# Product 4 of the first layer by seven blocks of its own, and the sums of slots made by GpSimd

## The chip, the cores and the metric

The kernel runs on one core of one Trainium2 chip. Its time is the device time of one execution in microseconds; three runs are shown, and the median counts. Five engines work side by side [...]: TensorE (PE, its weight loads PEld), VectorE (DVE), ScalarE (ACT), GpSimd (POOL) and SyncE (SP), which here only issues transfers. Each engine takes its instructions in the order of the program.

## The reference

All data are float32. The input x has 4096 tokens of 512 numbers. Two quaternion products and a filter, which is one number per channel, come down to a 4 x 4 matrix per channel (`M` in the kernel) that mixes the four quarters of a token. The result goes into a mixture of 8 experts, each token to two of them:

```
xf = rotate(x)                                  # 4096 x 512
scores = softmax(xf @ gate_w.T); topv, topi = top_k(scores, 2)
gates = topv / sum(topv)
# every expert takes up to 1024 slots; tokens beyond that are dropped
h  = relu(de[e] @ fc1_w[e].T + fc1_b[e])        # 1024 x 2048, de[e]: slots of expert e
eo = h @ fc2_w[e] + fc2_b[e]                    # 1024 x 512
out = x + sum over the two experts of gate * eo
```

## The kernel before

A first part chooses the experts and makes the lists of slots. Then come 32 groups k = 4 e + g: expert e (0 to 7) and quarter g (0 to 3) of the 2048 hidden columns. Each group has a first layer (512 hidden columns for 1024 slots) and a second layer.

**Seven products for eight.** Both layers cut their matrices into 2 x 2 blocks and make seven block products instead of eight, after Winograd's form of Strassen's method. The factors are blocks or sums of blocks: sums of weights `s` (`left1`, line 132) and of slots `x` (`sums`, line 119, called by `Slots.factors`) for the first layer, and of second weights `t` (`right2`, line 177) and hidden values (`chain`, line 811) for the second. The sums of `left1`, `sums` and `right2` are made by GpSimd, those of `chain` by VectorE.

**Seven within one of seven.** In the first layer, products 1, 6, 3 and 2 are cut once more (`pair`, line 878): each is made of seven matmuls of 128 x 128 by 256 columns (`within`, line 835). Their sums of weights come from `left_sub` (line 146, GpSimd, four of 128 x 128 per product and group) and their sums of slots from `right_sub` (line 162, VectorE, four of 128 x 256 per product and expert). Products 0, 5 and 4 are plain: four matmuls of 512 columns each (`half`, line 856).

**Banks and additions.** Matmuls write into PSUM banks of 512 columns; the first layer has four (`bank1`). A term that several blocks of the result share is accumulated on in the same bank: TensorE writes term after term, and after each VectorE adds the bank to the blocks that want it (`add`, line 890; line 905 adds one bank to two pairs). TensorE may write the next term into a bank only when the addition before has read it. The blocks of the result lie in `beside` (three per group, two groups in turn: h11, h21, r12) and in one of five tiles `unused` (h22). `chain` then makes the three sums s1, s2, s4 that the second layer needs, in four additions of VectorE.

**The order of the work** is written by hand. `first_layers` is a generator with 14 units per group (0 to 3: products 0 and 5; 4 to 7: 1 and 6; 8, 9: 4; 10 to 13: 3 and 2), `second_layers` one with 7 steps for each half of the slots, so 14 per group as well. Group 0 is plain throughout (`layer1_plain`, line 940). The loop at line 1256 takes one unit and one step in turn, and the second layer is one group and about three units behind. After each unit and each step `turn` (line 789) issues so many closures from the list `background` as the table `PACE` (line 1244) says for this group and unit, and always one from the list `fetches`:

- `background` holds the additions of `chain` (put in front), the rotation of the next expert's slots (`Slots.steps`: transposes and multiply-adds of VectorE, 18 for each half), the weights of the slots (`weights`) and the stores (`store`: ScalarE weighs, GpSimd adds 128 x 512 and issues a scatter).
- `fetches` holds the transfers: gathers by GpSimd (choices, rows of the output, the next expert's slots), the load of the second bias, and the exchange between partitions (four transfers of SP each, line 707). `arrivals` (line 714) puts in gathers and exchanges of the next expert's slots in one go, with empty closures between.

Sums of weights and slots are issued in fixed units: `later` (line 1052) gives the units of `left_sub` and `right_sub`, `TURN_OF_SUM` those of `left1`; the four sums of `right2` are issued in steps 13 and 14, which fall in units 1 and 2 of the next group.

Of the kernel before, what the change touches and what calls it, by code (L numbers as in the profile page):

```python
# [39 lines left out]
P = 128  # L40
# [26 lines left out]
def kernel(  # L67
# [94 lines left out]
    def right_sub(pool, e, n, block):  # L162

        t = pool.tile([P, 4, HS], F32, tag=f"xsub{n}", name=f"xsub{n}_{e}")

        def b(c, h):
# [3 lines left out]
            lambda: V.tensor_tensor(t[:, 0], b(0, 1), b(0, 0), ALU.subtract),  # L170
            lambda: V.tensor_tensor(t[:, 1], b(1, 1), t[:, 0], ALU.subtract),
            lambda: V.tensor_tensor(t[:, 2], b(1, 1), b(0, 1), ALU.subtract),
            lambda: V.tensor_tensor(t[:, 3], b(1, 0), t[:, 1], ALU.subtract),
# [440 lines left out]
    beside = [hp.tile([P, 3, 2, HALF], F32, name=f"beside{i}") for i in range(2)]  # L614
    unused = [hp.tile([P, 2, HALF], F32, name=f"hidden{i}") for i in range(5)]
# [60 lines left out]
    class Slots:  # L676
# [37 lines left out]
        def arrivals(self, half):  # L714

            n = PER if half == 0 else 2
            t = self.a if half == 0 else self.b
            for at in range(0, PER, n):
                for st in range(n):
                    yield lambda st=st, at=at: self.gather_ahead(t[:, st], half, at + st)  # L720
                yield from [lambda: None] * 2
                for b in range(QT):
                    yield lambda b=b, at=at: self.exchange(t, half, at, b)
                yield from [lambda: None] * 2
# [71 lines left out]
    def product2(out, st0, factors, n, first, tiles=range(2)):  # L796
# [11 lines left out]
        if st0 + 2 == PER and 1 in tiles and n in (2, 3, 4, 5):  # L808
            unused.append(factors[0][n])

    def chain(k, h22):


        h11, h21, r12 = (beside[k % 2][:, i] for i in range(3))
# [3 lines left out]
        def last():  # L818
# [7 lines left out]
            *[lambda: None] * (2 if k == NK - 1 else 0),  # L826
            last,
        ]

# [16 lines left out]
    def layer1(k, factors, subs):  # L846
# [5 lines left out]
        h11, h21, r12 = (h[:, i] for i in range(3))  # L852
# [25 lines left out]
        def pair(n, o, at, base, base_read):  # L878
# [3 lines left out]
            two = h[:, at : at + 2]  # L882
            t, u = bank1(f"t{n}_{k}"), bank1(f"u{n}_{k}")
            halves = t.rearrange("p (n s) -> p n s", n=2)

            def both(bank, i, first=False):
                within(bank[:, A], subs, n, i, first)
                within(bank[:, B], subs, o, i)
# [38 lines left out]
        for m in range(2):  # L927
            half(b[m], m, 4, True)
            V.tensor_tensor(h22[:, m], b[m], h21[:, m], ALU.add)
            if m == 1:  # L930
                from4(1)
                relu(h22)
# [379 lines left out]
```

## Time and profile before

| | |
|---|---|
| median of 3 runs | 1564.13 us (1563.52 to 1565.92) |
| the profiled execution | 1567.49 us |
| its span, first to last instruction | 1565.7 us |
| mean granted TensorE clock | 0.989 |
| VectorE: L892, 128x512, bank and SBUF | 248 of 687 ns |
| VectorE: L905, 128x1024, bank to two pairs | 62 of 1225 ns |
| VectorE: sums of slots L170, L171, 128x256 | 16 + 16 from x: 887 and 1247 ns; least 415 |
| GpSimd: L155 to L158, 128x128 | 463 to 830 ns |
| GpSimd: L137 to L140, 128x512 | 1272 to 1282 ns |
| GpSimd: L125 to L128 on x, 128x1024 | 2354 to 2360 ns |
| GpSimd: gather of rows L601, scatter L657 | 64 of 996, 64 of 1095 ns |

The busy time in the profile counts instructions of an engine without the issue of registers and semaphores; starts of successive matmuls, not their printed lengths, give TensorE's pace, since matmuls overlap. A line such as L837 is that of a helper, so groups are told apart by the tiles named. "A <- B" in the lists of waits says that A stood until B was done; such releasers are inferred.

### The profile page before, as it was taken

Reading aid. Unit: us, or ns where it says so; the run is one execution under the profiler, and the core shown is the slowest. Engines: PE = TensorE matmul, PEld = TensorE weight load, DVE = VectorE, ACT = ScalarE, POOL = GpSimd, SP = SyncE. Lnnn points to the kernel's source line nnn. Section 1 sums busy time; section 2 is a strip of 40 time slices with the busy share of each in tenths; the row PEclk is TensorE's granted clock in tenths of the full one; section 3 lists DMA queues with packets and bytes.
Section 4 is the critical chain, followed back from the end, with each engine's and each line's share of the span. In section 5 each row is a group of like instructions: output and inputs, shape, how many; then the busy total and the mean of one; then the engine's idle time right before and its main releaser. Section 6 shows DMA issues by size and latency. Waiting matters only on the chain.

```text
span 1565.7 us, 17505 instructions
## 1 busy us (share of the span) xinstructions
PE 1531.0 (98%) x6399; PEld 1186.9 (76%) x6399; DVE 1152.8 (74%) x1608; ACT 316.6 (20%) x446; POOL 1045.9 (67%) x1129
## 2 busy tenths in 40 slices
PE   5899999999999999999999999999999999999997
PEld 2677777877877777877877777887777877777776
DVE  6667887588866888578885888758886688866656
ACT  3222211211131211221122221221212211121110
POOL 1763687755977478865779567785687747886453
PEclk7899999999999999999999999999999999999999
DMA  8463113421335203441135311442123511321021
GB/s 325 150 215 101 55 61 122 121 81 55 96 106 144 65 28 114 124 118 55 54 95 166 96 55 32 137 130 86 55 79 115 145 41 55 114 94 67 0 82 53
DMA packets 79374, 152.18 MB, mean 97 GB/s; under 512 B 12022, under 2 KB 40950, under 8 KB 74168
## 3 DMA queue, kind: packets, MB, share of 16 engines
q1 hardware_dynamic: 56848, 90.24, 18.6%
q0 software_dynamic: 18048, 52.31, 10.8%
q10 hardware_dynamic: 4392, 8.52, 1.4%
q8 instruction: 50, 0.82, 0.2%
q14 instruction: 36, 0.29, 0.1%
HBM read 119.77 MB, written 25.23 MB: 93 GB/s over the span
## 4 chain that ended last, share of the span: by engine, by line
PE 87%; DVE 6%; DMA 2%; issue 2%; POOL 1%; another core or an unknown queue 1%; SPq 1%; POOLq 0%; DVEq 0%
PE a L800 26%; PE b L800 19%; PE t L837 13%; PE a L858 11%; PE u L837 7%; PE b L858 7%; PE b L837 2%; PE a L837 1%; DMA xb<-in_xt_dram 1%; DVE hidden L824 1%; DVE xa L771 1%; PE p L959 1%; DVE hidden L820 1%; SPq L707 1%
## 5 line engine op out<-in xcount | busy, mean ns | idle before, releaser
L800 PE MATMUL a<-t,hidden 128*128 128x256 f32 x1024 | 242.0, 379 | 0.1
L892 DVE TENSOR_TENSOR beside<-t,beside 128x512 f32<-128x512 f32 x248 | 170.3, 687 | 92.3 <-PE t L837 88.1
L800 PEld LDWEIGHTS a<-t,hidden 128*128 128x128 f32 x1024 | 194.5, 190 | 53.0 <-issue 27.5
L833 ACT ACTIVATE beside<-beside 128x1024 f32<-128x1024 f32 x62 | 65.5, 1057 | 556.8 <-DVE beside L892 535.1
L837 PE MATMUL t<-xsub,sub 128*128 128x256 f32 x496 | 128.1, 381 | 0.9 <-DVE beside L892 0.2
L800 PEld LDWEIGHTS b<-w,hidden 128*128 128x128 f32 x504 | 95.8, 190 | 39.0 <-issue 29.2
L800 PE MATMUL b<-w,beside 128*128 128x256 f32 x512 | 121.0, 379 | 0.6 <-DVE acc L1224 0.6
L800 PE MATMUL a<-t,beside 128*128 128x256 f32 x512 | 120.9, 379 | 0.0
L800 PE MATMUL a<-w,beside 128*128 128x256 f32 x512 | 120.9, 379 | 0.0
L800 PE MATMUL b<-t,hidden 128*128 128x256 f32 x504 | 119.1, 379 | 0.0
L800 PE MATMUL b<-w,hidden 128*128 128x256 f32 x504 | 119.1, 379 | 0.0
L800 PEld LDWEIGHTS b<-w,beside 128*128 128x128 f32 x512 | 97.2, 190 | 27.3 <-issue 15.8
L800 PEld LDWEIGHTS a<-w,beside 128*128 128x128 f32 x512 | 97.3, 190 | 26.4 <-issue 14.8
L858 PE MATMUL b<-x,s 128*128 128x512 f32 x248 | 116.5, 592 | 0.0
L858 PE MATMUL a<-x,s 128*128 128x512 f32 x248 | 116.5, 592 | 0.0
L858 PE MATMUL a<-xa,w 128*128 128x512 f32 x248 | 116.4, 592 | 0.0
L137 POOL TENSOR_TENSOR s<-w 128x512 f32<-128x512 f32 x31 | 39.5, 1274 | 112.5 <-PE b L858 112.5
L139 POOL TENSOR_TENSOR s<-w 128x512 f32<-128x512 f32 x31 | 39.7, 1282 | 109.7 <-PE t L837 109.6
L140 POOL TENSOR_TENSOR s<-w,s 128x512 f32<-128x512 f32 x31 | 39.4, 1272 | 107.5 <-PE t L837 96.7
L800 PEld LDWEIGHTS a<-t,beside 128*128 128x128 f32 x512 | 97.3, 190 | 13.2
L837 PEld LDWEIGHTS t<-xsub,sub 128*128 128x128 f32 x496 | 93.6, 190 | 16.3 <-DVE beside L892 3.4
L800 PEld LDWEIGHTS b<-t,hidden 128*128 128x128 f32 x504 | 95.8, 190 | 13.0
(228 smaller groups left out, 3084.9 us busy)
## 6 DMA issues: line engine op xcount, KB each, us to landing
w<-in_w_dram SPq DMA_DIRECT2D x64, 1024.0 KB
xb<-in_xt_dram SPq DMA_DIRECT2D x8, 1024.0 KB
out_dram<-in_x_dram ACTq DMA_DIRECT2D x1, 8192.0 KB
rows<-xa SPq DMA_DIRECT2D x112, 64.0 KB
rows<-xb SPq DMA_DIRECT2D x224, 32.0 KB
b<-in_b_dram POOLq DMA_DIRECT2D x8, 256.0 KB
c<-choice,slot_cho POOLq DMA_INDIRECT x64
rows<-out_dram,slot_tok POOLq DMA_INDIRECT x64
```

The source lines that it names most:

```text
L137: lambda: G.tensor_tensor(s[0], w[:, 1, 0], w[:, 1, 1], ALU.add),
L139: lambda: G.tensor_tensor(s[2], w[:, 0, 0], w[:, 1, 0], ALU.subtract),
L140: lambda: G.tensor_tensor(s[3], w[:, 0, 1], s[1], ALU.subtract),
L707: nc.sync.dma_start(slots_of[half][q * CW : (q + 1) * CW, at : at + t.shape[1], b * P : (b + 1) * P], t[b * CW : (b + 1) * CW, :, q * P : ...
L771: V.scalar_tensor_tensor(to, t, M[:, i, j : j + 1], to, ALU.mult, ALU.add)
L800: nc.tensor.matmul(out[m] if isinstance(out, list) else out[:, m], lhsT=factors[0][n][:, c, (st0 + m) * P : (st0 + m + 1) * P], rhs=factor ...
L820: V.tensor_tensor(s4, h21, s2, ALU.subtract)
L824: lambda: V.tensor_tensor(s2, s1, h11, ALU.subtract),
L833: nc.scalar.activation(h, h, AF.Relu)
L837: nc.tensor.matmul(out, lhsT=subs[0][n][i], rhs=subs[1][n][i], start=first, stop=True, skip_group_check=True,)
L858: nc.tensor.matmul(out, lhsT=factors[0][n][:, c, m * P : (m + 1) * P], rhs=factors[1][n][:, c, :], start=first and c == 0, stop=c == 1, sk ...
L892: V.tensor_tensor(to, halves, to, ALU.add)
```

## The change

- `layer1` is written out anew. Product 4 is made of its own seven blocks (`singles`, `within`): in units 8 to 11, in banks `b` and `t4`, whose terms go into both blocks that want them (h22 and r12) by additions of VectorE that read the same 256 columns twice (`add_to_both`). Products 3 and 2 follow in units 10 to 13, partly in the same units. Steps of two terms into one bank stand in front of one addition where the blocks allow it (`singles` of two products into `b`).
- `beside` holds four blocks per group (h11, h22, h21, r12) and `unused` three tiles. ScalarE copies the second half of h21 into h22.
- In `chain` the last addition (s4) is no longer put in `background` with the three others; it waits in `waiting` until product 2 of the group before has been issued.
- `right_sub` is made by GpSimd, and there is one for product 4 too, as there is a `left_sub`. Their units change, as do those of `left1`.
- `arrivals` becomes `arrive`: gathers and exchanges of the next expert's slots are put in at units of their own, by the table `ARRIVE`; from the second expert on, four gathers of half 0 at (g 0, unit 3), two of half 1 at (0, 6), the first exchange at (0, 13). The rotation is put in at (1, 7) and (2, 6).
- `PACE` changes, and group 1 takes the row of g=1.

```diff
--- before.py
+++ after.py
@@ -161,16 +161,17 @@
     def right_sub(pool, e, n, block):
+        G = nc.gpsimd
         t = pool.tile([P, 4, HS], F32, tag=f"xsub{n}", name=f"xsub{n}_{e}")
         def b(c, h):
             return block[:, c, h * HS : (h + 1) * HS]
         steps = [
-            lambda: V.tensor_tensor(t[:, 0], b(0, 1), b(0, 0), ALU.subtract),
-            lambda: V.tensor_tensor(t[:, 1], b(1, 1), t[:, 0], ALU.subtract),
-            lambda: V.tensor_tensor(t[:, 2], b(1, 1), b(0, 1), ALU.subtract),
-            lambda: V.tensor_tensor(t[:, 3], b(1, 0), t[:, 1], ALU.subtract),
+            lambda: G.tensor_tensor(t[:, 0], b(0, 1), b(0, 0), ALU.subtract),
+            lambda: G.tensor_tensor(t[:, 1], b(1, 1), t[:, 0], ALU.subtract),
+            lambda: G.tensor_tensor(t[:, 2], b(1, 1), b(0, 1), ALU.subtract),
+            lambda: G.tensor_tensor(t[:, 3], b(1, 0), t[:, 1], ALU.subtract),
         ]
         return [b(0, 0), b(1, 0), b(1, 1), t[:, 3], t[:, 0], t[:, 1], t[:, 2]], steps
@@ -611,8 +612,8 @@
-    beside = [hp.tile([P, 3, 2, HALF], F32, name=f"beside{i}") for i in range(2)]
-    unused = [hp.tile([P, 2, HALF], F32, name=f"hidden{i}") for i in range(5)]
+    beside = [hp.tile([P, 4, 2, HALF], F32, name=f"beside{i}") for i in range(2)]
+    unused = [hp.tile([P, 2, HALF], F32, name=f"hidden{i}") for i in range(3)]
     stored, turned_of = {}, {}
@@ -711,17 +712,17 @@
                     t[b * CW : (b + 1) * CW, :, q * P : (q + 1) * P],
                 )
-        def arrivals(self, half):
+        def arrive(self, half, part):
+
             n = PER if half == 0 else 2
             t = self.a if half == 0 else self.b
-            for at in range(0, PER, n):
-                for st in range(n):
-                    yield lambda st=st, at=at: self.gather_ahead(t[:, st], half, at + st)
-                yield from [lambda: None] * 2
-                for b in range(QT):
-                    yield lambda b=b, at=at: self.exchange(t, half, at, b)
-                yield from [lambda: None] * 2
+            at = part // 2 * n
+            if part % 2 == 0:
+                return [
+                    lambda st=st: self.gather_ahead(t[:, st], half, at + st) for st in range(n)
+                ]
+            return [lambda b=b: self.exchange(t, half, at, b) for b in range(QT)]
         def turn_squares(self, half, j, t):
             V.transpose(
@@ -805,13 +806,17 @@
                     stop=c == 1,
                     skip_group_check=True,
                 )
-        if st0 + 2 == PER and 1 in tiles and n in (2, 3, 4, 5):
+        if st0 + 2 == PER and 1 in tiles and n in (2, 4, 5):
             unused.append(factors[0][n])
-
-    def chain(k, h22):
-
-
-        h11, h21, r12 = (beside[k % 2][:, i] for i in range(3))
+            if n == 2 and waiting:
+                background.insert(0, waiting.pop())
+
+    waiting = []
+
+    def chain(k):
+
+
+        h11, h22, h21, r12 = (beside[k % 2][:, i] for i in range(4))
         s1, s2 = unused.pop(0), unused.pop(0)
         hidden[k] = [h11, h21, None, h22, s1, s2, r12]
@@ -823,9 +828,8 @@
             lambda: V.scalar_tensor_tensor(s1, r12, 0.0, h22, ALU.max, ALU.add),
             lambda: V.tensor_tensor(s2, s1, h11, ALU.subtract),
             lambda: V.scalar_tensor_tensor(r12, r12, 0.0, h11, ALU.max, ALU.subtract),
-            *[lambda: None] * (2 if k == NK - 1 else 0),
-            last,
         ]
+        (waiting if k else background).append(last)
     hidden = {}
@@ -875,64 +879,95 @@
                 nc.scalar.activation(h21[:, m], a[m], AF.Identity, bias=hi[:, m : m + 1])
             yield
-        def pair(n, o, at, base, base_read):
...
+        def singles(bank, n, first=False):
+            within(bank[:, A], subs, n, 1, first)
+            within(bank[:, B], subs, n, 2)
+
+        def both(bank, n, o, i, first=False):
+            within(bank[:, A], subs, n, i, first)
+            within(bank[:, B], subs, o, i)
+
+        def add(two, m, half, bank):
+            to = two[:, :, m, half]
+            V.tensor_tensor(to, bank.rearrange("p (n s) -> p n s", n=2), to, ALU.add)
+
+        def add_twice(two, bank):
             to = two[:, :, :, B]
-            term = u.rearrange("p (n s) -> p n s", n=2).unsqueeze(2).to_broadcast([P, 2, 2, HS])
+            term = bank.rearrange("p (n s) -> p n s", n=2).unsqueeze(2).to_broadcast([P, 2, 2, HS])
             V.tensor_tensor(to, term, to, ALU.add)
-            yield
-            both(t, 6)
-            add(1, B)
-            within(u[:, A], subs, n, 1, True)
-            within(u[:, B], subs, n, 2)
-            V.tensor_tensor(two[:, 0, 0], u, two[:, 0, 0], ALU.add)
-            yield
-            both(t, 3)
-            add(1, A)
-            relu(two[:, 0])
-
-        def from5(m):
-            nc.scalar.activation(h21[:, m], a[m], AF.Identity, bias=hi[:, m : m + 1])
-
-        def from4(m):
-            V.tensor_tensor(r12[:, m], b[m], r12[:, m], ALU.add)
-
-        yield from pair(1, 6, 0, a[0], lambda: from5(0))
+
+        def add_to_both(two, m, half, term):
+
+            to = two[:, :, m, half]
+            V.tensor_tensor(to, term.unsqueeze(1).to_broadcast([P, 2, HS]), to, ALU.add)
+
+        def add_pair(one, bank):
+            V.tensor_tensor(one[:, 0], bank, one[:, 0], ALU.add)
+
+
+
+        two = h[:, 0:3:2]
+        t, u = bank1(f"t1_{k}"), bank1(f"u1_{k}")
+        singles(a[0], 6)
+        nc.scalar.activation(h21[:, 0], a[0], AF.Identity, bias=hi[:, 0:1])
+        both(t, 1, 6, 0, True)
+        add(two, 0, A, t)
         yield
-        h22 = unused.pop(0)
-        b = [bank1(f"b{m}_{k}") for m in range(2)]
-        for m in range(2):
-            half(b[m], m, 4, True)
-            V.tensor_tensor(h22[:, m], b[m], h21[:, m], ALU.add)
-            if m == 1:
-                from4(1)
-                relu(h22)
-            yield
-        yield from pair(3, 2, 1, b[0], lambda: from4(0))
-        chain(k, h22)
+        both(t, 1, 6, 5)
+        add(two, 0, B, t)
+        both(u, 1, 6, 4, True)
+        add_twice(two, u)
+        yield
+        both(t, 1, 6, 6)
+        add(two, 1, B, t)
+        singles(u, 1, True)
+        add_pair(h11, u)
+        yield
+        both(t, 1, 6, 3)
+        add(two, 1, A, t)
+        relu(h11)
+        yield
+        nc.scalar.activation(h22[:, 1], h21[:, 1], AF.Copy)
+        two = h[:, 1:4:2]
+        b, t4 = bank1(f"b_{k}"), bank1(f"t4_{k}")
+        singles(b, 4, True)
+        V.tensor_tensor(h22[:, 0], b, h21[:, 0], ALU.add)
+        within(t4[:, A], subs, 4, 0, True)
+        add_to_both(two, 0, A, t4[:, A])
+        yield
+        within(t4[:, A], subs, 4, 5)
+        within(t4[:, B], subs, 4, 4)
+        add_to_both(two, 0, B, t4[:, A])
+        to = two[:, :, :, B]
+        term = t4[:, B].unsqueeze(1).unsqueeze(1).to_broadcast([P, 2, 2, HS])
+        V.tensor_tensor(to, term, to, ALU.add)
+        yield
+        three = h[:, 2:4]
+        t, u = bank1(f"t3_{k}"), bank1(f"u3_{k}")
+        singles(b, 2)
+        within(t4[:, A], subs, 4, 6)
+        add_to_both(two, 1, B, t4[:, A])
+        both(t, 3, 2, 0, True)
+        add_pair(r12, b)
+        add(three, 0, A, t)
+        yield
+        within(t4[:, A], subs, 4, 3)
+        add_to_both(two, 1, A, t4[:, A])
+        relu(h22)
+        both(t, 3, 2, 5)
+        add(three, 0, B, t)
+        both(u, 3, 2, 4, True)
+        add_twice(three, u)
+        yield
+        both(t, 3, 2, 6)
+        add(three, 1, B, t)
+        singles(u, 3, True)
+        add_pair(h21, u)
+        yield
+        both(t, 3, 2, 3)
+        add(three, 1, A, t)
+        relu(h21)
+        chain(k)
         yield
     PAIRS = (slice(0, 2 * P), slice(2 * P, 4 * P))
...
@@ -1023,8 +1057,26 @@
         left_f, w1_t = None, None
         w1_of = {}
         lefts, right_subs = {}, {}
-        TURN_OF_SUM = {8: 2, 9: 0, 10: 1, 13: 3}
+        TURN_OF_SUM = {8: 2, 11: 0, 12: 1, 13: 3}
         nxt = None
+        ARRIVE = (
+            {
+                (0, 5): [(0, 0)],
+                (1, 0): [(0, 1)],
+                (1, 2): [(1, 0)],
+                (1, 5): [(1, 1)],
+                (1, 9): [(1, 2)],
+                (1, 12): [(1, 3)],
+            },
+            {
+                (0, 3): [(0, 0)],
+                (0, 6): [(1, 0)],
+                (0, 13): [(0, 1)],
+                (1, 6): [(1, 1)],
+                (1, 10): [(1, 2)],
+                (1, 13): [(1, 3)],
+            },
+        )
         for k in range(NK):
             e, g = divmod(k, NG)
             if k + 1 < NK:
@@ -1055,13 +1107,19 @@
             if k:
                 for n, block, turns in (
-                    (2, left_f[2], (2, 2, 3, 3)),
-                    (3, w1_of[k][:, 1, 1], (4, 4, 5, 5)),
+                    (4, left_f[4], (2, 2, 3, 3)),
+                    (2, left_f[2], (4, 4, 5, 5)),
+                    (3, w1_of[k][:, 1, 1], (6, 6, 7, 7)),
                 ):
                     lefts[n], more = left_sub(k, n, block)
                     later(more, turns)
                 if k == 1 or g == 0:
-                    for n, turns in ((6, (1, 2, 2, 3)), (2, (4, 4, 5, 5)), (3, (6, 7, 8, 9))):
+                    for n, turns in (
+                        (6, (2, 2, 3, 3)),
+                        (4, (3, 4, 4, 5)),
+                        (2, (2, 4, 7, 10)),
+                        (3, (3, 5, 8, 10)),
+                    ):
                         right_subs[n], more = right_sub(xtp, e, n, xf[n])
                         later(more, turns)
                 if k == 1:
@@ -1077,13 +1135,15 @@
                 if k:
                     if i == 8 and k + 1 < NK:
-                        lefts[6], more = left_sub(k + 1, 6, left_n[6])
-                        later(more, (9, 10, 11, 12))
-                        lefts[1], more = left_sub(k + 1, 1, w1_of[k + 1][:, 0, 1])
-                        later(more, (10, 11, 12, 13))
+                        for n, block, turns in (
+                            (1, w1_of[k + 1][:, 0, 1], (8, 8, 9, 9)),
+                            (6, left_n[6], (9, 10, 10, 11)),
+                        ):
+                            lefts[n], more = left_sub(k + 1, n, block)
+                            later(more, turns)
                         if g == NG - 1:
                             right_subs[1], more = right_sub(xtp, e + 1, 1, xf_n[1])
-                            later(more, (8, 9, 9, 12))
+                            later(more, (8, 10, 10, 12))
                     for f in ahead[i]:
                         f()
                 if k == 0 and i == 2:
@@ -1096,9 +1156,9 @@
                     nc.scalar.dma_start(*(a.rearrange("(b r) d -> r b d", r=PT) for a in (out, x)))
                 if e + 1 < E:
-                    if (g, i) in ((0, 12 if e else 5), (1, 8)):
-                        fetches.extend(nxt.arrivals(g))
-                    if (g, i) in ((1, 11), (2, 9)):
+                    for part in ARRIVE[e > 0].get((g, i), ()):
+                        fetches.extend(nxt.arrive(*part))
+                    if (g, i) in ((1, 7), (2, 6)):
                         background.extend(nxt.steps(g - 1))
                 if k and left_n and i in TURN_OF_SUM:
@@ -1242,10 +1302,9 @@
     PACE = (
-        [(1, 1)] * 2 + [(0, 1)] * 4 + [(0, 0)] + [(0, 1)] * 5 + [(1, 1), (0, 0)],
-        [(1, 1)] * 4 + [(1, 1), (0, 2), (0, 0), (0, 1), (1, 1)] + [(0, 1)] * 3 + [(1, 1), (0, 0)],
-        [(1, 1)] * 2 + [(2, 1)] * 2 + [(1, 2), (0, 2), (0, 0), (0, 1), (1, 1)]
-        + [(0, 1)] * 3 + [(1, 1), (0, 0)],
+        [(1, 1)] * 2 + [(1, 1)] * 4 + [(0, 0)] + [(0, 1)] * 5 + [(1, 1), (0, 0)],
+        [(1, 1)] * 4 + [(1, 2), (0, 2), (0, 0), (0, 1), (0, 1), (0, 0), (1, 1), (0, 0), (1, 1), (0, 0)],
+        [(1, 1)] * 2 + [(2, 1)] * 2 + [(1, 2), (1, 1), (0, 0), (0, 1), (0, 1), (0, 0), (1, 1), (0, 0), (1, 1), (0, 0)],
     )
     with tc.manual_schedule():
@@ -1261,7 +1320,7 @@
                     going = True
                 k, i = now
-                turn(1 if k in (0, NK - 1) else PACE[0 if k == 1 else min(k % NG, 2)][i][n])
+                turn(1 if k in (0, NK - 1) else PACE[min(k % NG, 2)][i][n])
         while background:
             turn()
```

More of the change, by code (lines that the diff above doesn't have):

```diff
@@ L851, in layer1 @@
         h = beside[k % 2]
-        h11, h21, r12 = (h[:, i] for i in range(3))
+        h11, h22, h21, r12 = (h[:, i] for i in range(4))
         A, B = slice(0, HS), slice(HS, HALF)
@@ L876, in layer1 @@
             yield
-        def pair(n, o, at, base, base_read):
[L882 to L888, printed above, removed]
-            def add(m, half):
-                to = two[:, :, m, half]
-                V.tensor_tensor(to, halves, to, ALU.add)
-            within(base[:, A], subs, o, 1)
-            within(base[:, B], subs, o, 2)
-            base_read()
-            both(t, 0, True)
-            add(0, A)
-            yield
-            both(t, 5)
-            add(0, B)
-            both(u, 4, True)
+        def singles(bank, n, first=False):
+            within(bank[:, A], subs, n, 1, first)
+            within(bank[:, B], subs, n, 2)
@@ L923, in layer1 @@
-        yield from pair(1, 6, 0, a[0], lambda: from5(0))
-        yield
-        h22 = unused.pop(0)
-        b = [bank1(f"b{m}_{k}") for m in range(2)]
-        for m in range(2):
-            half(b[m], m, 4, True)
-            V.tensor_tensor(h22[:, m], b[m], h21[:, m], ALU.add)
-            if m == 1:
-                from4(1)
-                relu(h22)
-            yield
-        yield from pair(3, 2, 1, b[0], lambda: from4(0))
-        chain(k, h22)
+        def add_to_both(two, m, half, term):
+            to = two[:, :, m, half]
+            V.tensor_tensor(to, term.unsqueeze(1).to_broadcast([P, 2, HS]), to, ALU.add)
@@ L943, in layer1_plain @@
         lo, hi = (b1_sb[:, e, g * 4 + 2 * a : g * 4 + 2 * a + 2] for a in range(2))
-        h11, h21, r12 = (beside[k % 2][:, i] for i in range(3))
-        h22 = unused.pop(0)
+        h11, h22, h21, r12 = (beside[k % 2][:, i] for i in range(4))
         for half in range(2):
@@ L977, in layer1_plain @@
                 if half == 1 and done:
-                    chain(k, h22)
+                    chain(k)
                 if len(parts) == 1 or i % 2:
```

## The prediction

> **What bounds the kernel now.** I read the head of the page first, then TensorE's waits, then the order of time on TensorE, then the busy time by group, and last GpSimd's order of time, since most of what the change moves goes there.
>
> ```profile
> span 1565.7 us, 17505 instructions
> PE 1531.0 (98%) x6399; PEld 1186.9 (76%) x6399; DVE 1152.8 (74%) x1608; ACT 316.6 (20%) x446; POOL 1045.9 (67%) x1129
> ```
>
> TensorE is busy for 98% of the span. The list of its own waits (total us, times, longest) holds start-up and almost nothing else:
>
> ```profile
> PE lt L359 <- DMA xb<-in_xt_dram: 12.7, 7, 6.8
> ...
> PE b L837 <- DVE hidden L929: 1.4, 1, 1.4
> ```
>
> So the time is TensorE's number of columns, and whatever makes it wait is added in full. Its order of time gives the price (start us, us, engine, line; the printed us overlap in the pipeline, so I take differences of starts; one float32 matmul is two records):
>
> ```profile
> 405.35 1.88 PE L858 MATMUL a<-xa,w 128*128 128x512 f32 x4
> ...
> 432.08 1.88 PE L858 MATMUL b<-x,s 128*128 128x512 f32 x4
> 433.79 1.89 PE L800 MATMUL a<-t,hidden 128*128 128x256 f32 x8
> 435.52 1.88 PE L858 MATMUL b<-x,s 128*128 128x512 f32 x4
> 437.24 1.89 PE L800 MATMUL b<-w,hidden 128*128 128x256 f32 x8
> 438.96 0.59 PE L837 MATMUL b<-xb,s 128*128 128x256 f32 x2
> 439.39 0.59 PE L837 MATMUL b<-xb,sub 128*128 128x256 f32 x2
> ...
> 451.91 1.88 PE L858 MATMUL a<-xa,w 128*128 128x512 f32 x4
> ```
>
> One group k (14 units of layer 1 laced with 14 steps of layer 2) takes 451.91 - 405.35 = 46.56 us. Two matmuls of 512 columns take 433.79 - 432.08 = 1.71 us, one of 256 takes 0.43 us, a step of layer 2 (four of 256) 1.73 us. Busy time by group (stretch: us, then PE, PEld, DVE, ACT, POOL):
>
> ```profile
> 405.40:451.90 46.50, 46.50 (x193) 36.43 (x192) 35.55 (x49) 9.69 (x14) 37.02 (x38) 1.00 0.33 107
> 451.90:498.50 46.60, 46.60 (x194) 36.51 (x193) 26.90 (x35) 12.20 (x18) 37.79 (x43) 1.00 0.49 142
> 498.50:545.00 46.50, 46.38 (x191) 35.78 (x190) 39.71 (x51) 9.00 (x14) 21.43 (x26) 1.00 0.25 73
> ```
>
> The first is group k=8, the first group of an expert (g=0). There GpSimd has 37 busy us of 46.5, and its DMA issues have gaps of about 0.3 us besides. This is the place that decides, so here it is in order of time:
>
> ```profile
> 405.10 2.36 POOL L128 TENSOR_TENSOR x<-xa,x 128x1024 f32<-128x1024 f32 x1
> 407.42 2.25 POOL L125 TENSOR_TENSOR t<-w 128x512 f32<-128x512 f32 x1
> ...
> 414.82 0.46 POOL L156 TENSOR_TENSOR sub<-sub,s 128x128 f32<-128x128 f32 x1
> 415.24 2.25 POOL L128 TENSOR_TENSOR t<-w,t 128x512 f32<-128x512 f32 x1
> ...
> 428.44 0.95 POOL L601 DMA_INDIRECT rows<-out_dram,slot_tok  x1 [0.30 <-issue]
> 429.70 0.95 POOL L601 DMA_INDIRECT rows<-out_dram,slot_tok  x1 [0.30 <-issue]
> 430.64 0.61 POOL L1121 DMA_DIRECT2D b<-in_b_dram  x1
> ...
> 440.75 1.27 POOL L673 TENSOR_TENSOR rows<-acc,rows 128x512 f32<-128x512 f32 x1 [1.99 <-ACT acc L671]
> 442.30 1.02 POOL L657 DMA_INDIRECT out_dram<-rows,slot_add  x1 [0.28 <-POOL rows L673]
> ```
>
> The reader is to see that GpSimd enters the group 2.1 us late with the expert's last sum (L128), works without a pause up to b2's load, which ends at 431.25 (25.9 us into the group), and takes its work strictly in program order.
>
> **The change part by part.**
>
> *Product 4.* Out go two units of two 512-column matmuls, 2 x 1.715 = 3.43 us; in come seven of 256 columns, 7 x 0.431 = 3.02. That is 0.41 us per group, and 31 groups (k=1 to 31) give **12.7 us**. This is all that the change can gain, as TensorE has no other idle time to give back. With it unit starts in a group become, counted from its start: U8 26.7, U9 29.7, U10 32.3, U11 36.2, U12 40.1, U13 43.55, end 46.1.
>
> *VectorE.* Four additions of 512 for product 4 become six of 512 and one of 1024 into both users: 2 x 0.69 + 1.23 = +2.6 us per group. The sums of slots leave: twelve in g=0, four in g=3. In g=2 VectorE then stands at 42.3 of 46.1 us. A bank takes its next step only after its addition has read it, and a layer-2 step (1.73 us) lies between. Walking units 8 to 13 with one background addition of 0.74 us in unit 7, VectorE finishes the first addition of product 4 about 3.0 us after U8, where unit 9 starts after 3.02. So that wait is about 0.1 us with its release, in some 23 groups with background: 3 us in all, between 0 and 30. In units 10 to 13 I find 0.3 us or more to spare. ACT gets one copy of 512 (0.69 us by L869) per group, hidden in its 36 idle us. SP issues the same transfers; the exchange of half 0 still waits for stores, which I place about 9 us into g=1, and ends 3 us before VectorE's first transpose wants it.
>
> *GpSimd: price of a sum of slots.* No row shows 128x256 there. Rows of 128x128 (0.455), 128x512 (1.27) and 128x1024 (2.355) lie on one line, which gives 0.73 long and about 0.70 from start to start. [...]
>
> *GpSimd in g=0, experts 1 to 6.* Units 12 and 13 multiply products 3 and 2 by the third and fourth sums of `right_subs`; the fourth are issued in unit 10. In program order these stand before the last of them: what is left of L128, 2.1 us; four sums of the second weights, 4 x 1.24 = 5.0; nineteen sums of weights (`left_sub` for 4, 2, 3, 1 and three of 6), 19 x 0.42 = 8.0; sixteen sums of slots, 11.2; one sum of `left1`, 1.2; twelve gathers (four of the next expert's slots, now queued at unit 3 in front of the eight rows), 12 x 1.225 = 14.7; b2's load 0.6; one more gather 1.3; one store, addition and scatter, 1.27 + 0.28 + 1.0 = 2.55. Sum: 46.6 us. To it comes what the four long SBUF additions of VectorE (L823, L824, L825, L820) take from GpSimd. An undisturbed row is
>
> ```profile
> 545.34 1.27 POOL L125 TENSOR_TENSOR t<-w 128x512 f32<-128x512 f32 x1
> ```
>
> against 2.25 above. In k=11 the four sums of `t` and four of `sub` took 10.66 us, against 6.6 undisturbed; in k=10 such an excess was 3.1; I take 3.5. Check on k=8 itself: its work up to 25.9, counted in the same way, is 20.9, excess 5.0, with VectorE's sums of slots still beside it. So the last sum is ready at **50.1**, and TensorE wants it at 43.55: it stands 6.5 us, in six groups **39 us**. In k=28 there are no gathers for a next expert, 4.9 + 1.3 less: 43.9, a wait of 0.4. In k=1 no rows, stores or b2 are in the queue, and the last sum comes in time by about 4 us.
>
> The third sum of product 3 (unit 8) is ready at 35 to 39, wanted at 40.1: no wait. Everything behind shifts too. After the wait, sum 1 of `left1` for the next group is ready 6.7 us into g=1 and wanted (product 5, unit 2) at 6.9; the second sum of `t` at 13 to 15, wanted at 15.4. Two us in all for these, between 0 and 10. In g=1 GpSimd has six gathers less and catches up.
>
> **Sum**: -12.7 + 39 + 0.4 + 3 + 2 = +32 us on the span of 1565.7. The profiled execution took 1567.5 and the median of the runs is 1564.1, so I put the 32 us on the median: **1596 us**, 2.0% slower. A change under 0.2% (3 us) can't be told from none here.
>
> **The rivals.**
> - *The queue is in time* (faster): 1564.1 - 12.7, or up to 5 more: **1551 to 1556**. For it speaks that groups g=1 and g=2 have room and that the four gathers leave the start of g=1. Against it is that even with no excess the queue ends at 46.6, three us late. The end turns where the wait is 2.1 us per expert (12.7 / 6), the last sum at 45.65. Chance 0.14.
> - *VectorE becomes the bound* in units 8 to 11 where the rotation runs beside: 1 to 1.5 us in each of 23 groups, 23 to 35 more, with the GpSimd wait about **1625**; alone 1580. For it: 92% busy in g=2; against: background is set to nothing in units 9, 11 and 13. Chance 0.08.
> - *The backlog spreads*: sums for g=1 late by 2 us and the exchange, which waits for the late scatters, holds VectorE's transpose: about 5 us more per expert, **1630**. Against: margins of 0.2 to 3 us as worked out above. Chance 0.10.
> - The main case has 0.68.
>
> **The numbers.** The main case's own ends: wait 3 us (no excess) gives 18 + 1 - 12.7 + 2 = +8, **1572**; the rule's price (+2) with the excess of 5.0 (+1.5) gives 10 us, 60 + 4 - 12.7 + 5, **1620**. The range 1569 to 1620 leaves out the first rival and the upper parts of two others, 0.2 together. Faster 0.14, same 0.03 (the wait lands at about 2 us), slower 0.83.
>
> **What would show it.** In the profile after: TensorE's waits name POOL `xsub` at the `t` matmuls of unit 13, about 6.5 us each, six times, in groups 4, 8, ..., 24; GpSimd without a pause from the start of g=0 into g=1, at or above 90% there; 128x256 sums of about 0.73 us; groups g=2 and g=3 at 46.1 us. Wrong would be: sums of 0.5 us, gathers that cost GpSimd under 1 us each, or VectorE named as releaser at the `t4` matmuls more often than POOL.

## The result, and the profile after

The changed kernel takes **1622.65 us** (median of 4 runs, 1620.65 to 1622.88), the kernel before, in the same comparison, 1565.03 (1563.52 to 1567.59). The ratio is **1.0364, 95% interval 1.0346 to 1.0382**: slower by 57.6 us where 32 were forecast. The time is 2.65 us above the range.

The head of the page of the changed kernel, and two lines of its list of TensorE's waits (total us, times, longest us):

```profile
span 1621.1 us, 18219 instructions
...
PE 1538.7 (95%) x6585; PEld 1235.3 (76%) x6585; DVE 1161.9 (72%) x1573; ACT 332.0 (20%) x477; POOL 1207.6 (74%) x1413
```

```profile
PE t L841 <- POOL xsub L174: 38.8, 6, 7.1
...
PE t L841 <- DVE beside L902: 10.7, 1, 10.7
```

The first wait is the predicted one, at its place and size: 39 us, six times. The second was not predicted. And the two are together 49.5 us, while the span grew by 55.4 although the change also gives time back: the waits cost more than they last. The period of a group, start to start of product 0 (worked out from TensorE's order of time), shows where the time is:

| us per group | before | after |
|---|---|---|
| group k=1 | 43.45 | 55.36 |
| k=4, 8, ..., 24 (g=0, experts 1 to 6) | 46.56 | 55.3 to 56.1 |
| other full groups to k=27 | 46.56, with six of 47.11 to 47.13 | 46.35 to 46.49 |
| k=28 | 46.56 | 46.53 |
| the last two | 46.65, 46.56 | 46.17, 46.15 |

Six groups and group 1 are slow; all others are faster than before, and the last ones by the whole predicted 0.41 us. Here is k=8, which starts at 425.46, first TensorE's order of time around the wait, then GpSimd's:

```profile
467.29 1.89 PE L801 MATMUL b<-t,hidden 128*128 128x256 f32 x8
475.56 1.22 PE L841 MATMUL t<-xsub,w 128*128 128x256 f32 x2 [6.38 <-POOL xsub L174]
476.58 1.06 PE L841 MATMUL t<-xsub,s 128*128 128x256 f32 x2
477.43 3.62 PE L801 MATMUL a<-t,beside 128*128 128x256 f32 x8
480.85 2.08 PE L862 MATMUL a<-xa,w 128*128 128x512 f32 x4
```

```profile
425.27 2.37 POOL L128 TENSOR_TENSOR x<-xa,x 128x1024 f32<-128x1024 f32 x1
...
470.09 1.28 POOL L674 TENSOR_TENSOR rows<-acc,rows 128x512 f32<-128x512 f32 x1
471.77 1.02 POOL L658 DMA_INDIRECT out_dram<-rows,slot_add  x1 [0.41 <-POOL rows L674]
473.09 0.99 POOL L695 DMA_INDIRECT xb<-in_xq_dram,slot_tok  x1 [0.30 <-issue]
474.11 0.73 POOL L174 TENSOR_TENSOR xsub<-xb,xsub 128x256 f32<-128x256 f32 x1
474.79 0.72 POOL L174 TENSOR_TENSOR xsub<-x,xsub 128x256 f32<-128x256 f32 x1
```

The last sum ends at 475.5, **50.0 us into the group; forecast was 50.1**. But look at what follows the wait. A matmul of 256 columns (two records) takes 476.58 - 475.56 = 1.02 us, the next 0.85, where 0.43 is the pace, and a step of layer 2 takes 480.85 - 477.43 = 3.42 instead of 1.73. TensorE runs at half speed. The busy time by stretch of the changed kernel shows a granted clock of 0.50 there (us, then busy PE, PEld, DVE, ACT, POOL with counts, the granted TensorE clock, DMA share, GB/s):

```profile
467.59:471.01 3.42, 1.59 (x8) 1.06 (x6) 0.59 (x1) 0.00 (x0) 3.38 (x6) 1.00 0.61 162
471.01:474.42 3.41, 0.00 (x0) 0.00 (x0) 0.00 (x0) 0.00 (x0) 2.67 (x4) 1.00 0.47 145
474.42:477.83 3.41, 2.27 (x5) 1.85 (x6) 0.15 (x1) 0.00 (x0) 3.23 (x6) 0.50 0.28 77
477.83:481.25 3.42, 3.42 (x9) 2.70 (x8) 0.70 (x2) 1.06 (x1) 3.13 (x4) 0.50 0.48 152
481.25:484.66 3.41, 3.41 (x13) 2.26 (x12) 2.77 (x3) 0.69 (x1) 3.13 (x3) 1.00 0.01 1
```

The stretches are chosen so that the clock changes only at their ends: it halves at 474.42, 5.2 us after the last matmul, and is back at 481.25, two stretches of 3.41 us later. TensorE works 5.7 us of that at half speed and so loses half of it, 2.8. All six waits bring a half clock, and worked out in this way each loses 2.8 to 2.9 us; the periods, less the wait and the 46.4 us of a group without it, give 2.6. The instants at which the clock halved, 112.61 us in group 1 first and 1252.66 last, lie 48, 58, 57, 57, 57 and 57 times 3.4133 us apart, to some hundredths of a us (1140.05 us for all 334): in this trace they lie on one grid, wherever the waits fall. In the five waits from k=8 on, the stretch of the grid that ends at the halving has no work of TensorE at all, in that of k=4 0.96 us; e3 and e11 below show how much work there can be in it.

Now the second wait, in group 1, from the changed kernel's orders of time of SP's queue, VectorE and TensorE:

```profile
95.00 20.34 SPq L708 DMA_DIRECT2D rows<-xa  x16
```

```profile
117.05 0.73 DVE L728 STREAM_TRANSPOSE xps<-rows 128x512 f32<-128x512 f32 x1 [10.73 <-DMA rows<-xa]
117.68 0.67 DVE L934 TENSOR_TENSOR beside<-b,beside 128x512 f32<-128x512 f32 x1
118.45 0.69 DVE L902 TENSOR_TENSOR beside<-t,beside 128x512 f32<-128x512 f32 x1
```

```profile
119.29 2.05 PE L841 MATMUL t<-xsub,sub 128*128 128x256 f32 x4 [10.68 <-DVE beside L902]
```

VectorE reached the first transpose of the rotation, had to stand 10.7 us for the exchange, and the bank additions of product 4 stood behind it. The exchange of half 0 takes SP 20.3 us here, where later experts take 11. Its sixteen transfers are no slower than those: they add up to 9.7 us. The rest is one stand after the sixth transfer, which the merged line hides and the list of SP's waits names, in the changed kernel and then in the kernel before:

```profile
SPq L708 <- DMA out_dram<-in_x_dram: 10.0, 1, 10.0
```

```profile
SPq L707 <- DMA out_dram<-in_x_dram: 13.7, 1, 13.7
```

That is the copy of x (8 MB) into the output, issued at 56.9 us. In the kernel before the exchange ended even later (at 118.6), but the transpose was due later too, and VectorE stood only 1.4 us before it:

```profile
121.39 0.73 DVE L727 STREAM_TRANSPOSE xps<-rows 128x512 f32<-128x512 f32 x1 [1.44 <-DMA rows<-xb]
```

### The profile page after: what moved, and what is told of

The parts are those of the page before. It is cut to its first block, busy times and chain, and to the rows that moved or that the text cites. A ratio compares the mean times of both kernels' runs of the same rounds, so it can differ in the third digit from the quotient of the medians.

```text
span 1621.1 us, 18219 instructions
## 1 busy us (share of the span) xinstructions
PE 1538.7 (95%) x6585; PEld 1235.3 (76%) x6585; DVE 1161.9 (72%) x1573; ACT 332.0 (20%) x477; POOL 1207.6 (74%) x1413
## 5 line engine op out<-in xcount | busy, mean ns | idle before, releaser
L892 DVE TENSOR_TENSOR beside<-t,beside 128x512 f32<-128x512 f32 x248 | 170.6, 688 | 137.7 <-PE t L841 134.4
L801 PE MATMUL a<-t,beside 128*128 128x256 f32 x1024 | 252.4, 391 | 0.1
L801 PEld LDWEIGHTS a<-t,beside 128*128 128x128 f32 x1024 | 201.9, 197 | 42.4 <-issue 14.1
L841 PE MATMUL t<-xsub,sub 128*128 128x256 f32 x682 | 181.1, 385 | 10.7 <-DVE beside L902 10.7
L841 PEld LDWEIGHTS t<-xsub,sub 128*128 128x128 f32 x682 | 127.4, 191 | 33.8 <-issue 11.0
L801 PE MATMUL a<-t,hidden 128*128 128x256 f32 x512 | 121.0, 379 | 0.0
L137 POOL TENSOR_TENSOR s<-w 128x512 f32<-128x512 f32 x31 | 39.6, 1276 | 91.3 <-PE t L841 91.3
L801 PEld LDWEIGHTS a<-t,hidden 128*128 128x128 f32 x512 | 97.5, 190 | 13.0
L658 POOL DMA_INDIRECT out_dram<-rows,slot_add x64 | 74.2, 1159 | 36.8 <-DVE rows L653 17.5
L902 DVE TENSOR_TENSOR beside<-t,beside 128x512 f32<-128x512 f32 x124 | 85.1, 686 | 17.6 <-PE t L841 14.4
L155 POOL TENSOR_TENSOR sub<-w 128x128 f32<-128x128 f32 x62 | 36.5, 589 | 69.9 <-PE u L841 69.6
```

Of the source, the lines that this page charges most:

```text
L137: lambda: G.tensor_tensor(s[0], w[:, 1, 0], w[:, 1, 1], ALU.add),
L155: lambda: G.tensor_tensor(t[:, 0], b(1, 0), b(1, 1), ALU.add),
L658: nc.gpsimd.indirect_dma_start(out=out_of[st], out_offset=bass.IndirectOffsetOnAxis(ap=slot_add[:, s : s + 1], axis=0), in_=self.rows[st], ...
L801: nc.tensor.matmul(out[m] if isinstance(out, list) else out[:, m], lhsT=factors[0][n][:, c, (st0 + m) * P : (st0 + m + 1) * P], rhs=factor ...
L841: nc.tensor.matmul(out, lhsT=subs[0][n][i], rhs=subs[1][n][i], start=first, stop=True, skip_group_check=True,)
L892: V.tensor_tensor(to, bank.rearrange("p (n s) -> p n s", n=2), to, ALU.add)
```

## The experiments

The main theory: GpSimd's queue before the last sum of slots, with the clock on top, costs some 9 us in each of six groups, and the early rotation 12 us in group 1. The first rival: the lateness is a matter of place, and a better order cures it. The second: it is the load from the start of g=0 on, so that work which is moved only waits elsewhere. The third: product 4's new scheme itself costs time on VectorE. None of these kernels leaves out any of the computation. The kernel before, in the three comparisons, took 1565.13 (e1 to e4), 1564.63 (e5 to e8) and 1567.14 us (e9 to e11).

**e1_order: the last sums in front of the stores and gathers.**

```diff
-                        (2, (2, 4, 7, 10)),
-                        (3, (3, 5, 8, 10)),
+                        (2, (2, 4, 7, 8)),
+                        (3, (3, 5, 7, 8)),
```

> The same work for every engine as in the changed kernel; only the last two sums of slots of products 2 and 3 are issued in units 7 and 8 instead of 8 and 10 (GpSimd still has them all). Theory 1, place in the queue: the six waits of unit 13 (38.8 us) go, and with them the half clock after each; the six groups g=0 took 54.6 us more than the others, so 1622.7 - 54.6 = 1568 us, groups g=0 at about 46.4 us. Rival, load: GpSimd has too much to do in g=0 whatever the order, so another sum comes late in its place and a wait of 5 to 6 us per expert stays, 1610 us or more.

Measured: **1635.80 us, ratio 1.0459 (1.0441 to 1.0476)**, so no cure at all. g=0 is at 46.15 us as hoped, but g=1 rose to 55.7 to 58.5. The list of TensorE's waits, then the one at k=9:

```profile
PE a L862 <- POOL s L138: 52.0, 6, 9.4
```

```profile
492.52 3.51 PE L862 MATMUL a<-x,s 128*128 128x512 f32 x4 [8.79 <-POOL s L138]
```

The place of the wait moved to the second sum of weights for product 5, unit 2 of the next group, and it became longer. GpSimd has no pause from the start of g=0 to there, and its whole lack on this stretch is about 9 us; in the changed kernel the stop in unit 13 and the slow stretch after it, 6.4 + 2.8 us, cover it (the sum ends at 486.25, product 5 starts at 487.94). "Place" falls for this order, and "load" stands.

**e2_first: in group 1 the rotation four units later.**

```diff
-                    if (g, i) in ((1, 7), (2, 6)):
+                    if (g, i) in ((1, 11 if e == 0 else 7), (2, 6)):
...
-                turn(1 if k in (0, NK - 1) else PACE[min(k % NG, 2)][i][n])
+                pace = {11: (0, 1), 12: (2, 1), 13: (1, 1)}.get(i) if k == 1 else None
+                turn(1 if k in (0, NK - 1) else (pace or PACE[min(k % NG, 2)][i])[n])
```

> The same work; only in group 1 (the first expert) the rotation of the next expert's slots is put in at unit 11 instead of 7, its six steps in units 11 to 13. Theory: the one wait of 10.7 us in group 1 comes from VectorE's first transpose, which stands in its queue until the exchange of slots has landed, at about 117 us; with the transpose behind that time the group takes 43 to 44 us instead of 55.4: 1622.7 - 12 = 1611 us. Rival: the exchange itself holds up something else in group 1 (the late exchange of half 1, the weights' loads behind it in SP's queue), and the wait moves to group 2: 1620 us or more.

Measured: **1623.10 us, 1.0372 (1.0355 to 1.0389)**: nothing. VectorE's wait went, but the group took 57.12 us, because GpSimd stood in the same group for the exchange that follows in SP's queue, that of half 1:

```profile
PE t L841 <- POOL xsub L174: 50.3, 7, 11.6
```

```profile
129.43 0.96 POOL L695 DMA_INDIRECT xb<-in_xq_dram,slot_tok  x1 [18.04 <-DMA rows<-xb]
130.69 0.95 POOL L695 DMA_INDIRECT xb<-in_xq_dram,slot_tok  x1 [0.30 <-issue]
131.66 0.73 POOL L174 TENSOR_TENSOR xsub<-xb,xsub 128x256 f32<-128x256 f32 x1
132.34 0.72 POOL L174 TENSOR_TENSOR xsub<-x,xsub 128x256 f32<-128x256 f32 x1
```

The gather of the second part of half 1 lands in the tile that the exchange still empties. It stood 18 us, and the last sums of slots behind it.

**e3_store: one store of g=0 a unit later**, so that TensorE stands for less than the 5.2 us after which the clock halved in k=8 (about 3 us less in front of the sum).

```diff
-        [(1, 1)] * 2 + [(1, 1)] * 4 + [(0, 0)] + [(0, 1)] * 5 + [(1, 1), (0, 0)],
+        [(1, 1)] * 2 + [(1, 1)] * 4 + [(0, 0)] + [(0, 1)] * 2 + [(0, 0)] + [(0, 1)] * 2 + [(1, 1), (0, 0)],
```

> The same work; the first store of an expert is issued one unit later, behind the last sums of slots, which takes 3.0 us (one addition, one scatter and gaps) from in front of them. Each wait of 6.5 us should become 3.5. Theory 2, a fixed loss: TensorE's clock goes to half only when it has stood for about 5.1 us, so waits of 3.5 leave it at full: 6 x (3.0 + 2.6) = 34 us less, 1589 us, granted clock about 0.985 in the profile and no stretch at 0.50 in the groups g=0. Rival, in proportion: half the wait takes half the loss, 6 x (3.0 + 1.2) = 25 us less, 1597 us. Rival, none: the clock has nothing to do with the waits, 6 x 3.0 = 18 us less, 1605 us.

Measured: **1612.74 us, 1.0307 (1.0287 to 1.0328)**. The waits fell to 3.7 us (3.5 was worked out), but the half clock stayed in all six. Stretches on the clock's grid around the waits at k=8 and k=20, same columns:

```profile
464.10:467.52 3.42, 2.42 (x12) 1.79 (x10) 1.25 (x2) 0.00 (x0) 2.98 (x6) 1.00 0.53 149
467.52:470.93 3.41, 0.74 (x3) 0.68 (x4) 0.00 (x0) 0.00 (x0) 3.19 (x5) 1.00 0.49 159
470.93:474.34 3.41, 3.41 (x9) 2.66 (x8) 0.69 (x1) 1.06 (x1) 2.96 (x4) 0.50 0.26 77
474.34:477.76 3.42, 3.42 (x13) 2.27 (x12) 2.95 (x3) 0.69 (x1) 3.27 (x4) 1.00 0.20 77
...
1044.28:1047.69 3.41, 1.10 (x6) 0.62 (x4) 0.11 (x1) 0.00 (x0) 3.07 (x7) 1.00 0.61 171
1047.69:1051.11 3.42, 2.04 (x5) 1.68 (x6) 0.00 (x0) 0.00 (x0) 3.24 (x6) 0.51 0.44 120
1051.11:1054.52 3.41, 3.41 (x10) 2.69 (x9) 0.69 (x1) 1.06 (x1) 3.13 (x4) 0.50 0.41 127
1054.52:1057.93 3.41, 3.41 (x14) 2.25 (x13) 2.94 (x3) 0.69 (x1) 3.13 (x3) 0.99 0.07 26
```

At k=8 matmuls resumed at 470.19, and the clock halved at 470.93, **when TensorE was busy again**; of the stretch that ended there it had been busy for 0.74 us. After one full stretch at half clock (1.7 us lost) it was back. At k=20 the wait is as long, but lies otherwise on the grid: after a stretch with 1.10 us of work the clock was at half, after one with 2.04 of work it still was, and the loss is 2.8. So my fixed threshold of 5.1 us of standing was wrong; what these halvings go with is the busy share of a stretch of the grid. Besides, 0.5 to 3.0 us came back in each following g=1 (46.9 to 49.4 us), as "load" says.

**e4_later: the last sums one unit later**, to see whether the loss of clock grows with the wait.

```diff
-                        (2, (2, 4, 7, 10)),
-                        (3, (3, 5, 8, 10)),
+                        (2, (2, 4, 7, 11)),
+                        (3, (3, 5, 8, 11)),
```

> The same work; the last sums of slots of products 2 and 3 are issued one unit later (11 instead of 10), behind two sums of weights, a gather and a store, 4.7 us. Each wait should grow from 6.5 to about 11.2 us. Theory 2, a fixed loss: the half clock after a wait lasts as long as before, so 6 x 4.7 = 28 us more, 1651 us. Rival, in proportion: the loss grows with the wait, 6 x (4.7 + 1.9) = 40 us more, 1662 us.

Measured: **1651.58 us, 1.0556 (1.0535 to 1.0577)**, as expected. The six waits of about 11 us lose 1.7 to 2.5 us each by the clock (half the work done at half clock), less than those of 6.4: more of the slow stretches falls into the standing itself. With e3: 3.7 us lose 1.7 to 2.8; 6.3 to 7.1 lose 2.8 to 2.9; 11 lose 1.7 to 2.5. **The loss is a price per wait, not a share of it.**

**e5_vector: the sums of slots on VectorE, product 4 as changed.**

```diff
-            lambda: G.tensor_tensor(t[:, 0], b(0, 1), b(0, 0), ALU.subtract),
+            lambda: V.tensor_tensor(t[:, 0], b(0, 1), b(0, 0), ALU.subtract),
```

and so for all four steps of `right_sub`.

> One part of the change undone alone: the sums of slots are made by VectorE again, at the changed kernel's own units; all else as changed. Theory 1a (after the reordering run: it is GpSimd's load between the start of g=0 and the second unit of g=1, not one sum's place): 16 x 0.70 = 11 us leave that stretch, about 7 were missing, so the waits of the six groups g=0 and of what follows in g=1 go, and their half clock: 54.6 us less, 1568 us; the wait of 10.7 us in group 1 (VectorE behind a transfer) stays. Rival, VectorE is late instead: it takes twelve sums of 0.4 to 1.5 us in g=0 and four in g=3 beside more additions, waits of several us per expert name DVE xsub or beside, 1590 us or more.

Measured: **1575.84 us, 1.0069 (1.0054 to 1.0085)**. All g=0 groups are at 46.15 to 46.28. Group 1 stays slow (58.0 us), so its loss belongs to what e5 keeps of the change (product 4, the new units of transfers and rotation), not to the moved sums. What was not expected are seven waits in g=3, where VectorE has the next expert's sums again:

```profile
PE t L841 <- DVE beside L902: 12.7, 2, 12.5
PE t L841 <- DVE beside L943: 7.4, 7, 1.1
```

**e6_first2: e2's edit, and the gathers and exchange of half 1's second part moved from group 1 to group 2**; the sums stay on GpSimd.

```diff
-                (1, 9): [(1, 2)],
-                (1, 12): [(1, 3)],
+                (2, 1): [(1, 2)],
+                (2, 3): [(1, 3)],
```

> The same work as changed; in group 1 the rotation comes at unit 11 as in the run before, and the two gathers of the second part of half 1, which stood 18 us in GpSimd's queue until the exchange before them had been done, come at unit 1 of group 2 (their exchange at unit 3). Theory: these two are all that stops group 1; it takes 43 to 44 us instead of 55.4, 1622.7 - 12 = 1611 us. Rival: as in the run before, the late exchange stops something else in groups 1 or 2, 1618 us or more.

Measured: **1608.07 us, 1.0280 (1.0264 to 1.0296)**. Group 1 takes 42.70 us instead of 55.36: the loss in group 1 is the exchange's, first through VectorE's transpose and, once that is moved, through GpSimd's gather. The six waits (38.7 us) stay.

**e7_move: the kernel before, with its sums of slots on GpSimd alone.**

```diff
-            lambda: V.tensor_tensor(t[:, 0], b(0, 1), b(0, 0), ALU.subtract),
+            lambda: nc.gpsimd.tensor_tensor(t[:, 0], b(0, 1), b(0, 0), ALU.subtract),
```

and so for all four steps.

> One part of the change done alone on the kernel before: its sums of slots by GpSimd, at their old units; product 4 plain, transfers as before. Theory 1a: GpSimd gets 12 x 0.70 = 8.4 us in g=0, where it stood 6.3 us; what is left over may delay the second sum of the second weights in g=1 by 0 to 1.5 us: 1565 to 1575 us. Rival, the move alone is what costs: waits of 6 us and half clock in each expert as in the changed kernel, 1610 us or more.

Measured: **1561.76 us, 0.9982 (0.9973 to 0.9991)**. The six groups of 47.11 us are gone: 6 x 0.55 = 3.3 us, where the medians differ by 2.9. With twelve sums of slots in g=0, without the four of product 4 and its four sums of weights, and with the next expert's four gathers still in g=1, GpSimd is in time.

**e8_both: e5 and e6 together** (product 4 as changed, the sums on VectorE, groups 1 and 2 mended).

> The sums of slots by VectorE and the two moves in groups 1 and 2 together, product 4 by seven blocks. Theory: both kinds of wait are gone, groups of 46.15 to 46.4 us: 1622.7 - 54.6 - 12 = 1556 us, 0.6% faster than before; all of it from product 4 (31 x 0.41 = 12.7 us less about 5 of small waits for VectorE). Rival: VectorE's work in g=0 and g=3 takes the gain, 1565 us or more.

Measured: **1560.82 us, 0.9974 (0.9964 to 0.9983)**. TensorE's list of waits holds `DVE beside L943: 7.7, 7, 1.1` still; each g=3 takes 47.65 us (one 48.0), so the time is 5 us above the theory's.

**e9_one: e8, but the sums for product 1 (those of g=3) on GpSimd.**

```diff
-        G = nc.gpsimd
+        G = nc.gpsimd if n in (1,) else V
```

where the four steps are issued by `G` again.

> As the run with sums by VectorE and the two moves in groups 1 and 2, but the four sums of slots of product 1, issued in g=3 for the next expert, by GpSimd; the other sixteen by VectorE. In that run the groups g=3 took 47.65 us, 1.3 of it one wait for VectorE in unit 10, beside two of these sums. Theory: they are what makes VectorE late there; g=3 falls to 46.4, seven times 1.27 = 9 us: 1560.8 - 9 = 1552 us, 0.8% faster than before. Rival: the wait is that of the additions of product 4 and the rotation, and stays: 1560 us.

Measured: **1554.28 us (1553.81 to 1555.76), 0.9915 (0.9900 to 0.9929)**, the best of all. Its page:

```profile
span 1554.0 us, 18191 instructions
...
PE 1518.3 (98%) x6585; PEld 1219.8 (78%) x6585; DVE 1206.0 (78%) x1701; ACT 332.3 (21%) x477; POOL 1122.9 (72%) x1285
```

Every group from k=2 takes 46.1 to 46.4 us. No wait of the first layer on GpSimd is left. So product 4's new scheme does give nearly what the columns promise (46.15 us per group), when four sums per expert move, not sixteen more in g=0.

**e10_two and e11_three: products 1 and 6, and 1, 6 and 4 on GpSimd**, `n in (1, 6)` and `n in (1, 6, 4)` in the same line, to find how much room g=0 has.

> As e9_one, but product 6's sums by GpSimd too: eight of twenty there, four of them in g=0. Load theory: about 7 us were missing to GpSimd in g=0 with sixteen sums there (11.2 us); with four (2.8 us) it is 1.4 us ahead: no wait, 1552 us as e9_one, within 2 us. Rival, any sum on GpSimd in g=0 makes a wait: 1560 us or more.

> As e10_two, but product 4's sums by GpSimd as well: eight sums (5.6 us) in g=0. Load theory: 1.4 us are missing per expert; waits of 1 to 2 us for GpSimd in g=0 or at the start of g=1, too short for the half clock: 1552 + 6 x 1.4 = 1560 us, between 1555 and 1566. Rival, it is not a sum of loads and the room is larger: 1552 us; or the half clock comes with these waits too: 1570 us or more.

Measured: **1559.77 us, 0.9948 (0.9930 to 0.9965)**, and **1589.25 us, 1.0132 (1.0111 to 1.0153)**, both above what was expected. TensorE's waits of the one, then of the other:

```profile
PE a L862 <- POOL s L138: 3.2, 6, 0.7
```

```profile
PE a L862 <- POOL s L138: 24.6, 6, 5.7
```

Of the forecasts for e11 it was the rival with the half clock (1570 us or more) that came. Four sums in g=0 are already 0.5 us too many by unit 2 of g=1, eight are 3.5 to 5.7 and all sixteen about 9 (e1). Each four add 2.8 us of work (4 x 0.70), so the room is a little over 2 us. I had counted about 4, from the wait in unit 13 alone: the place where it is tightest comes later. Five of e11's six waits also bring the half clock. The last one, 3.5 us at k=25, does not (that g=1 takes 49.94 us, the others 51.6 to 55.1), and it shows the other side:

```profile
1228.70:1232.11 3.41, 1.82 (x9) 1.26 (x7) 3.41 (x2) 0.69 (x1) 3.13 (x3) 1.00 0.06 23
1232.11:1235.52 3.41, 1.51 (x4) 0.79 (x5) 1.33 (x2) 0.00 (x0) 3.11 (x4) 1.00 0.16 62
1235.52:1238.93 3.41, 3.41 (x14) 2.25 (x13) 1.17 (x2) 0.69 (x1) 3.39 (x3) 1.00 0.20 77
...
655.27:658.68 3.41, 1.33 (x7) 0.82 (x5) 3.41 (x2) 0.33 (x1) 3.13 (x3) 1.00 0.00 0
```

The wait is cut by the grid into two stretches with 1.82 and 1.51 us of work, and the clock stays. The last line is the stretch before the clock halved in k=13 of the same kernel, with 1.33 us of work.

## Why the prediction was wrong in size

**Right.** The mechanism, its place and its count: the last sum ready at 50.1 us (50.0), 39 us in six waits (38.8), 0.4 us in k=28 (46.53 - 46.15 = 0.4). The rows of 128x128, 128x512 and 128x1024 gave the right price of a sum: 0.73 us (0.72 to 0.74 for nine in ten of the 160). The "rule's price (+2)" in the sum for 1620 is a term that no run shows; the runs show the 0.73 us of the rows in its place. The gain of 0.41 us per group is there to the last digit (46.15). VectorE's small waits are 46.37 - 46.15 = 0.2 us per group with background, some 5 us where 3 were forecast.

**The step that failed is the price of a wait**: "the time is TensorE's number of columns, and whatever makes it wait is added in full". A wait of this length is added in full and then 2.75 us more (between the 2.6 and 2.9 above), as the clock halves. Six times 2.75 is 16.5 us that no term of the sum held. The profile of before gave little sign of it. Inside the groups it has no wait of more than 1.4 us, and it shows the clock below full only in the first two of its 40 slices, in the start-up, where TensorE waits 12.7 us in all for its first data:

```profile
PEclk7899999999999999999999999999999999999999
```

**The second failed step is group 1.** "In k=1 no rows, stores or b2 are in the queue, and the last sum comes in time by about 4 us" looked at GpSimd's queue alone. The exchange was placed only for later experts ("ends 3 us before VectorE's first transpose wants it"); for the first one, where the rotation is now put in at unit 7 as well, it was not, and SP's stand for the copy of x was in no term. The price is 55.36 less the 43.45 - 0.41 that it would have been, 12.3 us: 10.7 of wait and 1.6 by the clock (10.2 us at half, most of them in the wait).

**A gain not seen**: the six groups that were 0.55 us longer in before, 3.3 us, are so no more; e7 shows that they went with the sums. And the wait of 1.4 us for `hidden` in the last group of before is gone.

The account: 32 + 16.5 + 12.3 - 3.3 - 1.4 = 56.1 us, against 57.6 in the medians and 55.4 in the spans. (VectorE's small waits, 2 more, and the 2 us forecast behind the wait, which did not come, cancel.)

**The rivals.** "The queue is in time" was read as a matter of 2.1 us per expert; in truth it needs some 9 us less of GpSimd's work between the start of g=0 and unit 2 of g=1, and of the other orders that were run e1 only moved the wait, and e3 gained 10 us of the 57.6. "VectorE becomes the bound" did not come. "The backlog spreads" has the time nearest to the result (1630), but not its cause: in the changed kernel g=1 stays at 46.4, because TensorE's own stop hides the backlog; it spreads where that stop is removed (e1, e3). The line "two us in all" for the sums behind the wait was therefore right only thanks to the wait.

Not settled: why the first exchange has to wait for the copy of x. That it does is in the traces: in all thirteen, the two kernels' and the eleven runs', its seventh transfer starts 0.3 to 0.5 us after the copy's last packet. No run left the copy out or placed it elsewhere.

## What to carry to other kernels

Price a new wait on TensorE's path at its length plus the half clock that follows: here 1.5 to 3.1 us for every wait of 3.5 us or more but one, and nothing for those up to 1.5 us (1.48 and 1.49 in e3, at a granted clock of 1.00). Of the ten waits of 3.5 to 3.7 us in e3, e4 and e11 one escaped that price. When work moves to an engine with idle time, add up its queue to every later due time, not to the one that is late first, and look at the first round of a loop on its own, as its queues hold other work. Here moving four sums per expert in place of all twenty turned 3.6% slower into 0.85% faster (with group 1 mended).

## What was not expected of the hardware

- In the groups, the clock's changes lie on a grid of 3.4133 us (1140.05 us for 334 in the changed kernel). After a stretch in which TensorE was busy for up to 1.37 us (40%, e3) the clock was halved in the next, after one with 1.51 (44%, e11) or more it was not; at half clock, it stayed there after up to 2.7 us of work in a stretch (e11) and was back after 3.0 (e1) or more. The halving came 2.1 to 5.3 us after the last matmul before the wait, in e3 up to 1.4 us after matmuls had resumed, and the half clock lasted whole multiples: 3.41, 6.83, 10.24 or 13.65 us. In the start-up the busy time of a stretch does not tell the two apart: in the changed kernel the clock halved after one with 2.78 us (from 23.86), and in the kernel before it stayed at half after one with 3.42 (from 26.03).
- A sum of 128x256 takes GpSimd 0.72 to 0.74 us nearly always (8 of 160 in the changed kernel took over 1 us). On VectorE it took 0.415 at least, but 1.24 in the median for those of `L171` from x in the kernel before. In e5, where VectorE made all 160, the median was 0.42, and 21 took over 1 us. So the undisturbed rows alone don't give the price of the move.
- In e2 a GpSimd gather whose landing tile was not free held up all that stood behind it in that queue for 18 us, though GpSimd itself was idle in that time.
- A transfer that had to wait held up SP's queue in the same way. The sixteen of the exchange took 5.1 + 6.1 us for k=9, and 20.3 us in group 1, of which 10.0 are one stand for the copy of x. A line of the merged order of time, as `95.00 20.34 ... x16`, can hide such a stand; the list of waits of that queue shows it.
